# Router tokens turned by transfers and VectorE, the projection evicted by ScalarE, and new ranks in the planner

## Chip, cores and metric

The kernel runs on one core of one Trainium2 chip. The metric is device time in microseconds (us) of one execution.

## What is computed

For 32 sequences of 512 tokens with 256 features, in float32: a pre-normalised attention layer with a residual, then a pre-normalised routed slot layer with a residual.

```python
x = x + attn(layernorm(x));  x = x + ffn(layernorm(x))

# attn
q = tanh(x @ W_charge.T + b_charge)[..., 0]
phi_c = mags * q[..., None] ** arange(5)                 # powers 0..4 of the charge
shell = x @ W_shell.T + b_shell;  shell = shell / norm(shell)
phi_s = concat([cos(shell @ omega.T + rff_bias), sin(...)]) * rff_scale
phi = (phi_c[..., :, None] * phi_s[..., None, :]).reshape(b, n, -1) @ W_combine.T
attn = softmax(where(causal, phi @ phi.T * T / temp, -inf))
out = (attn @ (x @ W_v.T + b_v)) @ W_out.T + b_out

# ffn (the slots S are the same for every sequence before the update)
h = gelu(concat([x, slot_mean]) @ w1.T + b1)
alpha = top-8 softmax of (h @ w2.T + b2) / (|tau| + 0.1), spread over 64 slots
slot_input = einsum('bts,btd->bsd', alpha, x) / alpha.sum(axis=1)
S_new = gru(slot_input, S)
out = einsum('bts,bsd->btd', alpha, S_new @ wv.T + bv) @ wo.T + bo
```

## The kernel before, in words

The work is cut into 16 groups (g = 0 to 15) of two sequences. A group's x is one tile of 128 partitions by 8 token tiles by 256 features. Each group goes through `features` (L827), `attention` (L1070), `router` (L1218) and `slots` (L1356). TensorE = PE, VectorE = DVE, ScalarE = ACT, GpSimd = POOL, and SP issues nearly all transfers.

- **features.** `statistics` (L716) takes means and variances on VectorE (L724) and finishes on GpSimd. The tokens are turned so that features lie on partitions (xT): in groups 0 and 1 by TensorE (pta, L792), in the others by loading x again in 32-token blocks (xb, `load_x`, L261) and turning the 32x32 blocks on VectorE (L814). TensorE projects (pf, L843) with one weight tile for shell, charge and value columns, 321 in all; for the re-laid tokens a re-laid copy of the weights, wfb, is made by eight transfers. VectorE evicts each product with the scale of the normalisation and all biases in one instruction (sv, L856). The charge is spread by GpSimd (qrep, L879), turned by TensorE (ptq, L900), passed through tanh (L908) and squared (L911) on ScalarE. The shell norm, projection (pp, L979), angle and sine (L1011) follow. The powers 1 to 4 of the charge are four multiplications at L1022, of 512 elements each: powers 1 and 3 on VectorE, 2 and 4 on GpSimd. pph (L1041) combines them, and VectorE makes phi (L1056).
- **attention.** Logits (pl, L1094), row minimum (L1123), exponentials (L1135), transposes (ptp, L1171), their eviction (prT, L1189), values (po, L1177), and the addition to x (L1206). The output projection is folded into the value weights.
- **router.** Statistics again, xm (the normalised tokens, L1228, ScalarE), the transposes ptb (L760, inside `transposed`, L750) with evictions by ScalarE (xmT, L772), the hidden layer ph (L1254), gelu (L1265), logits prr (L1279), their transposes prt (L1285), the eight largest (top and rest, L1310 and L1311), the subtraction of the largest (L1319), exponential (L1328), sums (L1335) and weights al on GpSimd (L1344).
- **slots.** psi (L1367) gathers tokens into slots, gi (L1381), the gates prz and pn (L1416), the new state hn on VectorE, ScalarE and GpSimd, then pv (L1503), py (L1523), the addition to x (L1537) and the store (L1542).

The order in which each engine runs is fixed before the launch by a planner (`Plan.order`, L135). Every step has a cost and, for transfers, a time to land. A step's rank is

```python
s.rank = s.g * STRIDE + s.at + DELAY[s.stage]
```

where `at` is the earliest start within its group and the stages are setup, features, attention, router and slots. The planner places the ready step that can start first, by rank where several can, and counts the free buffers of each tag in `SLOTS_OF`. Each engine, and SP as a queue of transfers, then runs its steps in that order; groups overlap, so that one stretch of TensorE holds pf of one group, po of the one before and psi of the one before that.

## Time and profile before

| | us |
|---|---|
| median of 3 runs (lowest, highest) | 747.95 (746.84, 750.34) |
| the profiled execution | 746.77 |
| its span, first to last instruction | 744.9 |

The profile is of that one execution. PE is matmul, PEld weight loading, which overlaps PE; a line such as L760 is a line of the kernel. In a row of groups the columns are busy time, mean ns of one instruction, and idle time before it with what ended it. In a row of one tile's instructions the three numbers are the shortest, median and longest duration in ns. The slices divide the span into 40 parts, each digit a busy share in tenths; PEclk is TensorE's granted clock in tenths. The mean granted clock is 0.973. Matmul durations overlap, because matmuls are pipelined: 64 runs of four transposes ptb have a busy sum of 34.4 us.

### The profile page before, as it was taken

To read this page: it belongs to the slowest core of one execution; us is meant where nothing else is said; L and a number is where in the kernel's file an instruction comes from. 1 tells how busy PE (TensorE), PEld (TensorE's weight loads), DVE (VectorE), ACT (ScalarE), POOL (GpSimd) and SP (SyncE) were. 2 spreads that over 40 slices of the span, in tenths; PEclk is the share of its full clock that TensorE was granted. 3 is DMA by queue.
4 is the path that set the end of the run, shared out by engine and by line. 5 is a ranking of instruction groups with operands and counts; after the bars stand their busy time and mean duration, and the time that the engine had idled before them with its cause. 6 is when DMAs were issued, how large, how long until landed. Compare 5 with 4: busy or idle time off the path is not lost.

```text
span 744.9 us, 12365 instructions
## 1 busy us (share of the span) xinstructions
PE 698.8 (94%) x4170; PEld 489.6 (66%) x4170; DVE 592.2 (79%) x1747; ACT 432.7 (58%) x872; POOL 266.6 (36%) x510
## 2 busy tenths in 40 slices
PE   4988999999999999999999999999999999989754
PEld 4756766776767677677667677677667676756432
DVE  4899758788888889897979899897979788676443
ACT  3235656567475747477585757577585756574520
POOL 6542632342524252341525253442524252402010
PEclk8989999999999999999999999999999999999967
DMA  7886202005070604142150604142030301010103
GB/s 190 225 156 139 56 2 58 1 19 153 1 170 0 165 7 113 58 81 91 35 136 1 166 5 113 57 89 84 1 114 1 114 1 57 0 58 1 58 4 110
DMA packets 99151, 53.76 MB, mean 72 GB/s; under 512 B 63088, under 2 KB 98256, under 8 KB 99088
## 3 DMA queue, kind: packets, MB, share of 16 engines
q1 hardware_dynamic: 97216, 52.02, 27.1%
q8 instruction: 33, 0.54, 0.3%
q10 hardware_dynamic: 1376, 0.62, 0.3%
q0 software_dynamic: 496, 0.33, 0.2%
q14 instruction: 30, 0.25, 0.1%
HBM read 35.85 MB, written 16.78 MB: 71 GB/s over the span
## 4 chain that ended last, share of the span: by engine, by line
PE 76%; DVE 11%; DMA 4%; ACT 3%; SPq 2%; POOL 2%; issue 1%; DVEq 0%; POOLq 0%; ACTq 0%
PE po L1177 17%; PE pf L843 13%; PE ph L1254 7%; PE ptp L1171 4%; PE psi L1367 4%; PE pl L1094 4%; PE prz L1416 4%; PE pph L1041 4%; PE py L1523 4%; PE ptb L760 2%; SPq L247 2%; PE prr L1279 2%; DVE rest L1311 2%; PE pv L1503 2%; PE pn L1416 2%
## 5 line engine op out<-in xcount | busy, mean ns | idle before, releaser
L1177 PE MATMUL po<-sv,prT 128*128 128x256 f32 x640 | 149.6, 380 | 1.2 <-ACT prT L1189 1.2
L1177 PEld LDWEIGHTS po<-sv,prT 128*128 128x128 f32 x640 | 116.8, 189 | 22.2 <-issue 4.7
L843 PE MATMUL pf<-wfb,xT 128*128 128x321 f32 x448 | 126.7, 436 | 0.0
L843 PEld LDWEIGHTS pf<-wfb,xT 128*128 128x128 f32 x448 | 83.0, 189 | 41.4 <-issue 5.9
L1228 ACT ACTIVATE xm<-x,lnb 128x256 f32<-128x256 f32 x128 | 65.7, 590 | 32.8 <-POOL lnb L745 31.2
L1022 POOL TENSOR_TENSOR tp<-tp,q 128x512 f32<-128x512 f32 x32 | 45.4, 1420 | 107.5 <-ACT tp L1011 106.2
L1135 ACT ACTIVATE pr<-lg,nm 128x256 f32<-128x256 f32 (+3 forms) x128 | 70.7, 555 | 17.3 <-DVE nm L1123 16.8
L1206 DVE SCALAR_TENSOR_TENSOR x<-po,den,x 128x256 f32<-128x256 f32 x128 | 58.6, 474 | 20.2 <-PE po L1177 19.6
L856 DVE SCALAR_TENSOR_TENSOR sv<-pf,lna,bias_f 128x321 f32<-128x321 f32 x128 | 64.2, 540 | 13.0 <-PE pf L843 12.9
L1189 ACT COPY prT<-ptp 128x384 f32<-128x384 f32 (+1 forms) x96 | 47.7, 516 | 42.5 <-PE ptp L1171 42.2
L1123 DVE CUSTOM_DVE_ANT_0 lg<-pl,mask 128x128 f32<-128x128 f32 (+3 forms) x128 | 57.2, 483 | 14.0 <-PE pl L1094 9.3
L1254 PE MATMUL ph<-xmT,w1x 128*128 128x512 f32 x128 | 61.5, 606 | 0.0
L1462 POOL TENSOR_TENSOR nn<-nn,rh 128x256 f32<-128x256 f32 x16 | 11.7, 729 | 139.2 <-DVE rh L1453 122.2
L724 DVE BATCH_NORM_STATS2 bna<-x 128x6 f32<-128x256 f32 x128 | 46.4, 409 | 12.3 <-DMA x<-in_x_dram 12.3
L1171 PE MATMUL ptp<-ident,pr 128*128 128x128 f32 x320 | 48.9, 275 | 2.4 <-ACT pr L1135 2.3
L879 POOL COPY qrep<-sv 128x128 f32<-128x128 f32 x64 | 19.6, 321 | 80.6 <-DVE sv L856 79.3
L724 DVE BATCH_NORM_STATS2 bnb<-x 128x6 f32<-128x256 f32 x128 | 47.4, 411 | 0.7
L1171 PEld LDWEIGHTS ptp<-ident,pr 128*128 128x128 f32 x320 | 38.1, 140 | 14.4 <-issue 4.3
L1094 PE MATMUL pl<-phi 64*128 64x256 f32 (+1 forms) x384 | 44.3, 359 | 0.0
L1537 DVE TENSOR_TENSOR x<-py,x 128x512 f32<-128x512 f32 x64 | 39.8, 678 | 5.3 <-PE py L1523 5.2
L1094 PEld LDWEIGHTS pl<-phi 64*128 64x128 f32 x384 | 31.2, 186 | 11.2 <-issue 5.1
L1041 PE MATMUL pph<-tp,wc 64*64 64x256 f32 x640 | 38.2, 381 | 0.0
(177 smaller groups left out, 1339.7 us busy)
## 6 DMA issues: line engine op xcount, KB each, us to landing
x<-in_x_dram SPq DMA_DIRECT2D x32, 512.0 KB, 4.9
out_dram<-x SPq DMA_DIRECT2D x64, 256.0 KB, 2.5
xb<-in_x_dram SPq DMA_DIRECT2D x112, 128.0 KB, 3.4
setup<-in_gru_whh_t_dram SPq DMA_DIRECT2D x1, 768.0 KB, 4.6
wih<-in_gru_wih_t_dram SPq DMA_DIRECT2D x1, 768.0 KB, 6.4
wfb<-wf SPq DMA_DIRECT2D x8, 40.1 KB, 2.5
setup<-in_W_v_dram ACTq DMA_DIRECT2D x1, 256.0 KB, 8.7
setup<-in_W_out_t_dram ACTq DMA_DIRECT2D x1, 256.0 KB, 8.8
```

The source lines that it names most:

```text
L724: lambda t=t: nc.vector.bn_stats(st()[:, t, :], src()[:, t, :]),
L843: nc.tensor.matmul(pf()[:, 0:NF], tile_()[:, k, c * P : (c + 1) * P], w[:, k, :], start=(k == 0), stop=(k == KD - 1),)
L856: lambda t=t, pf=pf: nc.vector.scalar_tensor_tensor(sv()[:, t, :], pf()[:, 0:NF], ln()[:, 1, t : t + 1], bias_f, ALU.mult, ALU.add,),
L1041: nc.tensor.matmul(phs[h]()[bb * COMB : (bb + 1) * COMB, 0:HT], wc[r, m, :], tp()[r, m, bb * HT : (bb + 1) * HT], start=(m == 0), stop=(m ...
L1094: nc.tensor.matmul(pls[bb]()[:, off[i] + lo : off[i] + lo + w], phi()[r, 0, q : q + P], phi()[r, 1, k : k + w], start=True, stop=True,)
L1123: nc.vector.tensor_tensor_reduce(out=lg()[:, c], in0=pls[bb]()[:, c], in1=mask[:, T - w : T], scale=1.0, scalar=TOP, op0=ALU.add, op1=ALU.min,
L1135: nc.scalar.activation(pr()[:, c], lg()[:, c], AF.Exp, bias=nm(), scale=-1.0, accum_out=den()[:, tiles.index(i), bb : bb + 1],)
L1171: nc.tensor.transpose(pt()[:, j : j + P], prs[bb]()[:, j : j + P], ident)
L1177: nc.tensor.matmul(po()[:, d * D : (d + 1) * D], pr_t()[:, lo : lo + P], sv()[:, bb * NT + j, C_V:NF], start=(j == 0), stop=(j == i),)
L1206: nc.vector.scalar_tensor_tensor(xt()[:, t, :], po()[:, d * D : (d + 1) * D], den()[:, d, bb : bb + 1], xt()[:, t, :], ALU.mult, ALU.add,)
L1228: lambda t=t: nc.scalar.activation(xm()[:, t, 0:D], xt()[:, t, :], AF.Identity, bias=ln()[:, 4, t : t + 1], scale=ln()[:, 1, t : t + 1],),
L1254: nc.tensor.matmul(ph(), w1x[:, k, :], tiles[k](), start=(k == 0), stop=(k == KD - 1))
```

## The change

- The router's tokens: xm is laid out in four feature quarters of 64, each with a column of ones. In groups 0 to 13, 16 transfers on SP for each of a group's two sequences move 32-partition pieces of xm into xmT (4 token tiles by 65 elements, 1,040 bytes a partition), and VectorE turns the 32x32 blocks in place, two instructions of 512 elements a sequence. ph then uses re-laid weights w1b (four more loads at the start), reads xmT in runs of 32 elements, and gelu writes its output in token order again. psi is 260 columns wide instead of 257. Groups 14 and 15 (`LAST_BY_TENSOR`) keep transposing on TensorE with evictions on ScalarE.
- The projection is evicted by ScalarE, with the scale alone. GpSimd adds the value bias to x (two instructions of 1024 elements a group; attention weights sum to one, so the bias passes through), VectorE adds the shell bias (two instructions a group), and the charge bias goes into the tanh.
- The four powers become two VectorE instructions of 1024 elements.
- The planner: twelve stages instead of five, each with two delays (the second for the last groups), ranks that mix the earliest start with the length of what follows (`LATE`), new constants, some costs, and fewer buffers for xT, xmT, row and half.

The diff, cut to its core:

```diff
@@ -54,8 +57,8 @@
-    "xT": 4,
-    "xmT": 4,
+    "xT": 3,
+    "xmT": 3,
@@ -64,17 +67,31 @@
-    "row": 8,
-    "half": 5,
+    "row": 6,
+    "half": 4,
 }
 HOP = 0.5
 TABLE = 1.28
-SWITCH = 2.0
-STRIDE = 26.0
-
-DELAY = {"setup": 0.0, "features": -32.0, "attention": -14.0, "router": -1.0, "slots": 3.0}
+SWITCH = 0.94
+STRIDE = 33.46
+LATE = 0.77
+
+DELAY = {
+    "setup": (0.0, 0.0),
+    "load": (17.9, 6.2),
+    "tokens": (0.9, -4.2),
+    "angles": (-26.7, -8.1),
+    "phi": (1.6, 1.1),
+    "weights": (5.2, 7.7),
+    "values": (-6.7, -0.6),
+    "normal": (23.4, 21.8),
+    "router": (17.0, -4.1),
+    "taken": (5.8, -10.8),
+    "gru": (31.9, -18.4),
+    "given": (38.2, -0.7),
+}
@@ -143,8 +160,23 @@
                 ),
                 default=0.0,
             )
+
+        for s in reversed(self.steps):
+            s.tail = (
+                s.cost
+                + s.land
+                + max(
+                    (o.tail + (HOP if o.eng != s.eng else 0.0) for o in s.next if o.g == s.g),
+                    default=0.0,
+                )
+            )
+        last = max(s.g for s in self.steps)
+        longest = max(s.tail for s in self.steps if s.rank is None)
+        for s in self.steps:
             if s.rank is None:
-                s.rank = s.g * STRIDE + s.at + DELAY[s.stage]
+                at = (1.0 - LATE) * s.at + LATE * (longest - s.tail)
+                delay, late = DELAY[s.stage]
+                s.rank = s.g * STRIDE + at + delay + late * max(0, s.g - last + 3)
         free = {e: 0.0 for e in ("PE", "DVE", "ACT", "POOL", "SP")}
         slots = {tag: [0.0] * n for tag, n in SLOTS_OF.items()}
         for s in self.steps:
@@ -613,6 +646,10 @@
+    w1q = a["w1_t"][0:D, :].rearrange("(q k i) n -> q i k n", q=NQ, k=KD)
+    l_w1b = [
+        load("SP", w1b[q * SQ : (q + 1) * SQ, :, :], w1q[q], 32, rank=30.0) for q in range(NQ)
+    ]
@@ -851,21 +860,48 @@
             s = add("PE", 1.1, project, done[c // 2] + w_done, [tile_, pf, sv])
             s_sv.append(
                 add(
-                    "DVE",
-                    0.42,
-                    lambda t=t, pf=pf: nc.vector.scalar_tensor_tensor(
-                        sv()[:, t, :],
-                        pf()[:, 0:NF],
-                        ln()[:, 1, t : t + 1],
-                        bias_f,
-                        ALU.mult,
-                        ALU.add,
+                    "ACT",
+                    0.47,
+                    lambda t=t, pf=pf: nc.scalar.activation(
+                        sv()[:, t, :], pf()[:, 0:NF], AF.Copy, scale=ln()[:, 1, t : t + 1]
                     ),
-                    [s, s_ln] + B_PF,
+                    [s, s_ln],
                     [pf, sv, ln],
                 )
             )
+        s_xb = [
+            add(
+                "POOL",
+                2.9,
+                lambda bb=bb: nc.gpsimd.tensor_tensor(
+                    xt()[:, bb * NT : (bb + 1) * NT, :],
+                    xt()[:, bb * NT : (bb + 1) * NT, :],
+                    bias_f[:, C_V:NF].unsqueeze(1).to_broadcast([P, NT, D]),
+                    ALU.add,
+                ),
+                [s_ln] + (x_t[bb][1][0] if g < BY_TENSOR else []) + B_PF,
+                [xt],
+            )
+            for bb in range(GB)
+        ]
+        s_sh = [
+            add(
+                "DVE",
+                0.4,
+                lambda bb=bb: nc.vector.tensor_tensor(
+                    sv()[:, bb * NT : (bb + 1) * NT, 0:SHELL],
+                    sv()[:, bb * NT : (bb + 1) * NT, 0:SHELL],
+                    bias_f[:, 0:SHELL].unsqueeze(1).to_broadcast([P, NT, SHELL]),
+                    ALU.add,
+                ),
+                s_sv[bb * NT : (bb + 1) * NT] + B_PF,
+                [sv],
+            )
+            for bb in range(GB)
+        ]
+
+        plan.stage = "angles"
@@ -903,12 +939,23 @@
                     ident,
                 )
-        s = add("PE", 0.44, charges_turned, s_rep + [s_ident], [qrep, ptq, qb])
-        s_qb = add(
-            "ACT", 0.6, lambda: nc.scalar.activation(qb(), ptq(), AF.Tanh), [s], [ptq, qb], "exp"
-        )
-        s_q2 = add(
-            "ACT", 0.6, lambda: nc.scalar.activation(q2(), qb(), AF.Square), [s_qb], [qb, q2]
+        s = add("PE", 0.44, charges_turned, s_rep + [s_ident], [qrep, ptq, tp])
+        s = add(
+            "ACT",
+            0.6,
+            lambda: nc.scalar.activation(
+                tp()[:, ORDER + 1, :], ptq(), AF.Tanh, bias=bias_f[:, C_Q : C_Q + 1]
+            ),
+            [s] + B_PF,
+            [ptq, tp],
+            "exp",
+        )
+        s_q = add(
+            "ACT",
+            0.6,
+            lambda: nc.scalar.activation(tp()[:, ORDER + 2, :], tp()[:, ORDER + 1, :], AF.Square),
+            [s],
+            [tp],
         )
@@ -1004,32 +1050,29 @@
             nc.vector.scalar_tensor_tensor(turn(), turn(), -ROUND, ang(), ALU.add, ALU.subtract)
         s = add("DVE", 1.05, nearest, s, [ang, turn])
-        s_tp = {}
-        s_tp[0] = add(
-            "ACT",
-            0.6,
-            lambda: nc.scalar.activation(tp()[:, 0, :], turn(), AF.Sin, scale=-TWO_PI),
-            [s],
-            [turn, tp],
-            "sin",
-        )
-
-        def power(eng, cost, m, by, s_by):
-            e = nc.vector if eng == "DVE" else nc.gpsimd
-            s_tp[m] = add(
-                eng,
-                cost,
-                lambda: e.tensor_tensor(
-                    tp()[:, m, :], tp()[:, m - 1 if by is qb else m - 2, :], by(), ALU.mult
-                ),
-                [s_tp[m - 1 if by is qb else m - 2], s_by],
-                [tp, by],
-            )
-
-        power("DVE", 0.75, 1, qb, s_qb)
-        power("POOL", 1.2, 2, q2, s_q2)
-        power("DVE", 0.75, 3, q2, s_q2)
-        power("POOL", 1.2, 4, q2, s_q2)
+        s_tp = [
+            add(
+                "ACT",
+                0.6,
+                lambda: nc.scalar.activation(tp()[:, 0, :], turn(), AF.Sin, scale=-TWO_PI),
+                [s],
+                [turn, tp],
+                "sin",
+            )
+        ]
+
+        for m in (1, 3):
+
+            def powers(m=m):
+                a, b = tp()[:, 0:1, :], tp()[:, ORDER + 1 : ORDER + 3, :]
+                if m == 1:
+                    a = a.to_broadcast([P, 2, T])
+                else:
+                    a, b = tp()[:, 1:3, :], b[:, 1:2, :].to_broadcast([P, 2, T])
+                nc.vector.tensor_tensor(tp()[:, m : m + 2, :], a, b, ALU.mult)
+
+            s_tp.append(add("DVE", 1.3, powers, [s_tp[-1], s_q], [tp]))
+        plan.stage = "phi"
@@ -1212,32 +1257,108 @@
                             ALU.add,
                         )
-                    s_x[t] = add("DVE", 0.42, added, [s_po, s_den], [po, den, xt])
+                    s_x[t] = add("DVE", 0.42, added, [s_po, s_den, s_xb[bb]], [po, den, xt])
         return s_x
...
+
+
+        by_tensor = g >= NG - LAST_BY_TENSOR
         xm = Lazy("xm", lambda: xms[g % len(xms)])
         al = lazy("al", f"al_{g}", [P, NT, GB, SLOTS])
+
...
         ln, s_ln = statistics(g, "b", xt, [xt], s_x)
+        ones = [s_one]
+        if by_tensor:
+            ones = [
+                add("POOL", 0.2, lambda: nc.gpsimd.memset(plain()[:, :, D : D + 1], 1.0), [s_one, s_ln], [xm])
+            ]
+
...
         s_xm = [
...
+            add("ACT", 0.51, lambda t=t: normalised(t), [s_ln] + ones, [xm, xt, ln])
             for t in range(GT)
         ]
-        xm_t = transposed(g, "b", xm, [xm], s_xm, "xmT")
+
+        xm_t, s_xmt = [], []
+        for bb in range(GB):
+            dst = lazy("xmT", f"xmT_{g}_{bb}", [P, NT * NT, EQ + 1])
+            xm_t.append(dst)
+            here = s_xm[bb * NT : (bb + 1) * NT]
+            done = []
+            if by_tensor:
...
+            else:
+
+
+                moved = [
+                    add(
+                        "SP",
+                        0.45,
+                        lambda bb=bb, q=q, b=b, dst=dst: nc.sync.dma_start(
+                            out=dst()[q * SQ : (q + 1) * SQ, b * NT : (b + 1) * NT, :],
+                            in_=xm()[b * SQ : (b + 1) * SQ, q, bb * NT : (bb + 1) * NT, :],
+                        ),
+                        here,
+                        [xm, dst],
+                        land=2.3,
+                    )
+                    for b in range(NT)
+                    for q in range(NQ)
+                ]
+                for h in range(2):
+
+                    def turn(h=h, dst=dst):
+                        n = NT * NT // 2
+                        v = dst()[:, h * n : (h + 1) * n, 0:EQ]
+                        nc.vector.transpose(v, v)
+
+                    done.append(add("DVE", 0.63, turn, moved, [dst]))
+            s_xmt.append(done)
+        plan.stage = "router"
@@ -1247,27 +1368,25 @@
...
-                    nc.tensor.matmul(
-                        ph(), w1x[:, k, :], tiles[k](), start=(k == 0), stop=(k == KD - 1)
-                    )
-
-            s = add(
-                "PE", 1.72, hidden, [xm_t[bb, k][1] for k in range(KD)] + [l_w1x], tiles + [ph, h_t]
-            )
-            s_h.append(
-                add(
-                    "ACT",
-                    0.6,
-                    lambda ph=ph, h_t=h_t: nc.scalar.activation(h_t(), ph(), AF.Gelu, bias=b1e),
-                    [s, s_b1e],
-                    [ph, h_t],
-                    "gelu",
-                )
-            )
+                    if by_tensor:
+                        w = w1x
+                        rhs = tile_().rearrange("p t e -> p (t e)")[:, k * T : (k + 1) * T]
+                    else:
+                        w = w1b
+                        rhs = tile_()[:, :, k * SQ : (k + 1) * SQ]
+                    nc.tensor.matmul(ph(), w[:, k, :], rhs, start=(k == 0), stop=(k == KD - 1))
+
+            def active(ph=ph, h_t=h_t):
+                src, dst = ph(), h_t()
+                if not by_tensor:
+                    src = src.rearrange("p (b c i) -> p b c i", b=NT, c=NT)
+                    dst = dst.rearrange("p (c b i) -> p b c i", b=NT, c=NT)
+                nc.scalar.activation(dst, src, AF.Gelu, bias=b1e)
+
+            s = add("PE", 1.72, hidden, s_xmt[bb] + [l_w1x] + l_w1b, [xm_t[bb], ph, h_t])
+            s_h.append(add("ACT", 0.6, active, [s, s_b1e], [ph, h_t], "gelu"))
             h_ts.append(h_t)
```

## The prediction, on record before the run

> **What bounds the kernel now.** I read the busy shares and the slices first, then the chain of waits, then busy time by stretches, then the groups with their forms.
>
> ```profile
> PE 698.8 (94%) x4170; PEld 489.6 (66%) x4170; DVE 592.2 (79%) x1747; ACT 432.7 (58%) x872; POOL 266.6 (36%) x510
> PE   4988999999999999999999999999999999989754
> PEclk8989999999999999999999999999999999999967
> PE 76%; DVE 11%; DMA 4%; ACT 3%; SPq 2%; POOL 2%; issue 1%; DVEq 0%; POOLq 0%; ACTq 0%
> ```
>
> TensorE is never below nine tenths between the first 90 us and the last 60, at a full clock, and three quarters of the chain is TensorE work. The middle falls only with TensorE's work; the two ends fall with latency.
>
> ```profile
> 279.00:372.00 93.00, 93.00 (x562) 66.14 (x561) 81.34 (x241) 59.79 (x120) 35.41 (x71) 1.00 0.29 75
> sum 372.00, PE 370.91 PEld 261.09 DVE 319.96 ACT 237.91 POOL 141.12; mean PE 92.73 PEld 65.27 DVE 79.99 ACT 59.48 POOL 35.28
> ```
>
> The columns are PE, PEld, DVE, ACT, POOL; the second line sums four stretches from 186 to 558 us. PE is idle 1.1 us of 372. The pph step of group 3 starts at 145.5 us and that of group 15 at 646.2, so a group takes 500.7/12 = 41.7 us. VectorE works 86% of it, 35.9 us; ScalarE 64%, 26.7; GpSimd 38%, 15.8. So VectorE is next in line.
>
> **The change part by part.** *Router transposes off TensorE.* Busy times of single matmuls overlap, so the price is the time a run holds the chain (start, us, what):
>
> ```profile
> 158.31 1.75 PE ptb L760 x16
> L772 ACT COPY xmT<-ptb 128x512 f32<-128x512 f32 x64 | 33.3, 593 | 0.6 <-PE ptb L760 0.4
> L814 DVE STREAM_TRANSPOSE xT<-xb 128x512 f32<-128x512 f32 x56 | 36.8, 686 | 0.0
> L247 SPq DMA_DIRECT2D wfb<-wf x8: 534/589/650, 19.9 to 24.4; - x8
> DMA to landing us min/median/max: 1.9/2.5/3.3
> ```
>
> Groups 0 to 13 lose 16 transposes each: 14 x 1.75 = **24.5 us of TensorE work**, all on the bounding engine; groups 14 and 15 keep theirs. ScalarE loses 4 x 0.52 = 2.1 us a group. VectorE gains 4 turns of 512 elements, at 36.8/56: 2.6 us. SP gains 32 transfers a group. The nearest row is wfb: also SBUF to SBUF, 32 partitions, 1.3 KB a partition against 1.04 here. At 0.589 us that is 18.8 us of SP; beside it stand 8 xb loads (5.0 us in the timeline), 4 stores (2.2) and 2 x loads (0.9): 26.9 of 41.7, so SP has room, but in order. In the new order 12 or 13 of item 1's 16 transfers stand before the stores of group g-2 and the rest behind them, so these wait for VectorE's last addition there; behind them wait the next xb and x loads.
>
> Does the longer road fit? In the new order TensorE has about 31 us of work between the last po of a group and its first ph. The road is addition and statistics 0.9, GpSimd's statistics 3.7, eight xm 4.1, 16 transfers 9.4, landing 2.5, two turns 1.3: 22 us. The second item's last transfers: from py to the second ph, TensorE has about 14 us, the road is 0.5 + four additions 2.5 + stores 2.2 + four transfers 2.4 + landing 2.5 + turns 1.3 = 11.4. Cover left: 9 and 2.6 us. The second is thin.
>
> ph now reads its moving side in pieces of 32 elements. No row shows that. Bounds: nothing, or a tenth of ph's 3.44 us a group (4.8 us in all); nothing can be gained, since the columns stay the same. I take nothing, because psi, pf and ph rows differ only with their columns. Permuted xm and gelu outputs on ScalarE: same answer, hidden by its idle 13 us.
>
> *Projection evicted by ScalarE.* Eight copies of 321 elements a group, nearest row prT 128x384 at 482 ns: +3.9 us on ScalarE, which comes to 26.7 - 2.1 + 3.9 = 28.5 us. VectorE loses 64.2/16 = 4.0 us and gains two additions for the shell bias; the shn row (128x256, 14.4/32) gives 0.9 us.
>
> *Powers and value bias.*
>
> ```profile
> L1022 POOL TENSOR_TENSOR tp<-tp,q x32: 1264/1310/1775, 47.5 to 640.5; 128x512 f32<-128x512 f32 x32
> L1022 DVE TENSOR_TENSOR tp<-tp,qb x16: 676/1322/1687, 46.3 to 639.5; 128x512 f32<-128x512 f32 x16
> L1022 DVE TENSOR_TENSOR tp<-tp,q x16: 691/1640/1653, 47.0 to 641.0; 128x512 f32<-128x512 f32 x16
> L1319 DVE TENSOR_TENSOR rl<-rl,top 128x512 f32<-128x512 f32 x16 | 11.6, 727 | 0.6
> L918 POOL TENSOR_TENSOR sq<-sv 128x256 f32<-128x256 f32 x32 | 19.7, 616 | 0.0
> ```
>
> The same multiplication takes VectorE 0.68 us at best and 1.64 when GpSimd multiplies beside it. The Trainium skill (SBUF — State Buffer, "Who interferes with whom") has the rule: a VectorE instruction with two SBUF inputs and a GpSimd instruction that reads SBUF shut each other out for a whole instruction. The rows agree with the waiting. For the powers this speaks for the change: VectorE loses 2.6 us (41.6/16) and gains two instructions of 1024 elements at 2 x 0.727 = 2.9, GpSimd loses 2.8. For the value bias the rule speaks against it: two additions of 1024 elements, 4 x 0.616 = 2.5 us each by the sq row, 2.8 by the powers row. In the new order they stand behind GpSimd's first statistics, when VectorE comes to the subtraction of the largest, the new state and the shell bias, all with two SBUF inputs. By the busy rows alone it costs VectorE nothing; by the rule one to two instructions wait up to 2.5 us a group. I take 1.3 to 2.5.
>
> VectorE's sum a group: 35.9 - 4.0 - 2.6 + 2.6 + 0.9 + 2.9 = 35.7, with the lock 37 to 38.2. TensorE's: 41.7 - 1.75 = 39.9. TensorE still bounds, but VectorE is at 93 to 96% and its queue is in order. For what then shows through (turns waiting for landings, the lock, fewer row and xT buffers) I take 0.33 us a group, **+4 us** over 12; the bounds are 0 and 5.
>
> *The planner.* Changes of TensorE's tile mode: 195 before, 189 after, so nothing there.
>
> Start: x of group 1 was loaded second and its transposes ran at 13.7 and 16.2 us, in time that TensorE had to wait anyway. Now its loads stand behind wfb, whose issue ends at 25 us; with 4.9 us to land, those transposes come at 30, behind pf of group 0: **+3.5 us**.
>
> End, by the timeline of TensorE:
>
> ```profile
> 678.22 3.62 PE L1177 MATMUL po<-sv,prT 128*128 128x256 f32 x16
> 704.40 0.60 PE L1285 MATMUL prt<-ident,rlT 128*128 128x128 f32 x4
> 716.42 0.66 PE L1391 MATMUL pt_hn<-ident,hn 128*128 128x128 f32 x2 [11.42 <-DVE hn L1477]
> ```
>
> From the last po (681.8) to the end are 63 us of group 15's own latency, with holes of 11.4 and 4.2 us. The new order puts more work under it: ph of group 14 (3.44), prz and pn of 13 (2.6) and half of ptb of 14 (0.87). **6.9 us** leave the stretch before. Against it ScalarE does the two gelu steps of group 14 inside the last chain and VectorE hn and x of 13: **+2 us**.
>
> Sum: -24.5 - 6.9 + 3.5 + 2 + 4 = -21.9 us. The profiled execution took 746.77 us (744.9 of span, 1.9 around it), 1.2 below the median of the runs. I take the difference from the median: 747.95 - 21.9 = 726.0.
>
> **The rivals.**
>
> *A, TensorE stays the bound (0.56): 726*, own range 716 to 735.
>
> *B, VectorE becomes the bound (0.18).* If the lock costs 5 us (each GpSimd addition holds one instruction for its whole length), VectorE has 40.7 us of work; with a few tenths of waits a group takes 41. Twelve groups then gain 0.7 each, 8.4, plus 1.4 net from the ends (6.9 - 3.5 - 2) less 2 at the edges of the middle: about 740. For it: 86% busy now. Against it: the sum above.
>
> *C, slower (0.10): the turned tokens come late.* VectorE waits at the turn of xmT with all its other work queued behind, then TensorE at ph. If landings beside xb loads take 4.9 us as for x, not 2.5, and VectorE is 3 us behind at the additions before the stores, the road of 11.4 becomes 16.8, 2.8 more than its cover. 12 x (2.8 - 0.33) = 30 us on A: 755. It ends slower from 2.2 us of lateness a group. Against it: the order leaves room on SP, and the wfb row landed in 2.5 us in a crowded stretch.
>
> *D, the ends gain more (0.13): 711.* TensorE is idle 16 us in the first 93 and 26 in the last 94; if group 1's late x costs nothing and the stalls before the last po (5 us) close, 726 - 3.5 - 5 - 4 - 2 = 711.5.
>
> *E, the change doesn't do what it says (0.03): ph costs more* for its short pieces, by up to a fifth: 14 x 0.69 = 10 us, 736.
>
> **How the numbers follow.** A measurement here tells 0.5% (3.7 us) from no change. A, D and E are faster; of B I give 0.14 to faster and 0.04 to no change; of C 0.01 to no change and 0.09 to slower. Faster 0.86, same 0.05, slower 0.09. The range goes from below D, 706, to where no change begins, 744; about 0.05 lies below and 0.13 above.
>
> **What would show it.** TensorE's busy time about 25 us lower and still full in the middle; a group at 40.2 us between pph steps; VectorE about 90% or more there; the tp row of VectorE near 1.45 us for 1024 elements; GpSimd's x row near 2.5; SP 0.5 to 0.6 per xmT transfer. Wrong: TensorE idle in the middle with VectorE's turn or DMA as releaser (C), VectorE full with rows of two SBUF inputs stretched (B), the ph row above 592 ns (E).

## The result and the profile after

| | us |
|---|---|
| before, median of 10 runs (lowest, highest) | 748.5 (746.8, 751.7) |
| after, median of 10 runs (lowest, highest) | 744.5 (740.7, 749.0) |
| after, the profiled execution, its span | 740.65, 738.9 |
| ratio of after to before, 95% interval | 0.9938 (0.9910 to 0.9966) |

The kernel became 4 us faster where 22 were forecast, and 744.5 lies just outside the range. The direction was right, the size was not. The profiled execution is the fastest of the ten after the change, 3.8 us below their median, and that of the kernel before lies 1.7 below its own, so the traces differ by 6 us where the medians differ by 4. Here are the busy shares, the slices and the chain of waits of the changed kernel:

```profile
PE 682.3 (92%) x3946; PEld 465.7 (63%) x3946; DVE 596.3 (81%) x1707; ACT 454.9 (62%) x939; POOL 291.1 (39%) x512
PE   5989898899999898999989998999989989899885
PEclk8998999999999999999999999999999999999997
PE 47%; DVE 19%; DMA 9%; ACT 9%; SPq 7%; POOL 5%; issue 3%; ACTq 0%; DVEq 0%; POOLq 0%
```

The work has moved as planned: TensorE is 16.5 us less busy, ScalarE 22.2 and GpSimd 24.5 us more, VectorE about as before. But TensorE has 8s in the middle, where it had none before, and its share of the chain fell from 76% to 47%. The same stretches of the middle, in the same columns, say it in numbers:

```profile
372.00:465.00 93.00, 87.37 (x521) 59.99 (x521) 84.43 (x224) 60.15 (x126) 38.82 (x64) 0.98 0.40 96
sum 372.00, PE 354.97 PEld 243.26 DVE 330.09 ACT 240.64 POOL 153.21; mean PE 88.74 PEld 60.82 DVE 82.52 ACT 60.16 POOL 38.30
```

TensorE idles 17.0 of 372 us, against 1.1 before, and the granted clock is 0.98 where it was 1.00. VectorE idles too, so neither engine is full. Between the pph steps of groups 3 and 13, a group takes 42.28 us, against 41.79 before and 40.2 in the forecast. By stretches, cut at the starts of those two steps and at the end of the last po:

| us | before | after | difference |
|---|---|---|---|
| start to pph of group 3 | 145.4 | 151.0 | +5.6 |
| ten groups | 417.9 | 422.8 | +4.9 |
| pph of group 13 to the last po | 118.5 | 109.0 | -9.5 |
| last po to the end | 63.1 | 56.1 | -7.0 |

The ends gained what was expected of them, more or less. The ten groups should have gained 15 us (41.7 to 40.2 each) and lost 4.9, so it is there that one has to look. The waits of TensorE over those 372 us of the changed kernel name what ended them (us in all, how often, the longest):

```profile
PE pt_hn L1521 <- DVE hn L1608: 11.8, 6, 2.2
PE pl L1138 <- ACT sv L865: 4.7, 3, 1.8
```

So TensorE stands at one place of its order, right behind the projection pf: at the transposes of the new state (pt_hn) in six groups and at the logits (pl) in three others. The timeline shows how hn came late (start, duration, what; a row may hold several instructions):

```profile
328.55 4.40 POOL L877 TENSOR_TENSOR x<-x,bias_f 128x1024 f32<-128x1024 f32 x2
```

```profile
328.82 2.28 DVE L1438 TENSOR_TENSOR rl<-rl,top 128x512 f32<-128x512 f32 x1
331.02 2.22 DVE L1607 SCALAR_TENSOR_TENSOR rh<-rz,rh 128x256 f32<-128x256 f32 x1
333.27 0.43 DVE L1608 SCALAR_TENSOR_TENSOR hn<-rh,nn 128x256 f32<-128x256 f32 x1
```

```profile
321.27 2.39 PE L1084 MATMUL pph<-tp,wc 64*64 64x256 f32 x40
323.59 0.66 PE L1404 MATMUL prt<-ident,rlT 128*128 128x128 f32 x4
324.08 7.74 PE L852 MATMUL pf<-wfb,xT 128*128 128x321 f32 x28
333.84 0.41 PE L1521 MATMUL pt_hn<-ident,hn 128*128 128x128 f32 x2 [2.02 <-DVE hn L1608]
```

GpSimd starts the first of its two additions 0.27 us before VectorE's subtraction rl, and rl, 0.73 us on average before, ends 0.55 us after the first addition; rh, 0.42 before, ends 0.28 us after the second. hn comes at 333.7, TensorE has been through with pf since 331.8. This row of the kernel before shows what rh took without the additions:

```profile
L1476 DVE SCALAR_TENSOR_TENSOR rh<-rz,rh 128x256 f32<-128x256 f32 x16 | 6.7, 416 | 3.3 <-POOL rh L1470 3.3
```

The chain of waits confirms the path, in order of time; an instruction that overlaps the one before it counts there only from where that one ends:

```profile
321.34 2.39 PE pph L1084 x40
323.73 1.40 DVE phi L1099 x4
325.13 0.15 DVE top L1429
...
328.82 2.28 DVE rl L1438
331.10 2.15 DVE rh L1607
...
333.27 0.44 DVE hn L1608
```

From pph over phi, the eight takes of the top, rl, rh and hn, VectorE's in-order queue makes one chain, although hn doesn't depend on phi or on the top. Beside it TensorE has only prt and pf to do.

### The profile page after: what moved, and what is told of

Same layout as the page of the kernel before. It is cut to its first block, busy times and chain, and to the rows that moved or that the text cites. A ratio compares the mean times of both kernels' runs of the same rounds, so it can differ in the third digit from the quotient of the medians.

```text
span 738.9 us, 12845 instructions
## 1 busy us (share of the span) xinstructions
PE 682.3 (92%) x3946; PEld 465.7 (63%) x3946; DVE 596.3 (81%) x1707; ACT 454.9 (62%) x939; POOL 291.1 (39%) x512
## 4 chain that ended last, share of the span: by engine, by line
PE 47%; DVE 19%; DMA 9%; ACT 9%; SPq 7%; POOL 5%; issue 3%; ACTq 0%; DVEq 0%; POOLq 0%
PE po L1222 12%; SPq L1341 5%; DMA x<-in_x_dram 5%; PE ph L1379 4%; PE pl L1138 4%; PE py L1655 4%; PE psi L1491 3%; PE prz L1547 3%; PE ptp L1216 3%; ACT xm L1291 3%; PE pf L852 3%; PE pph L1084 3%; DVE rest L1430 2%; PE pv L1635 2%; DVE rh L1607 2%
## 5 line engine op out<-in xcount | busy, mean ns | idle before, releaser
L1179 ACT ACTIVATE pr<-lg,nm 128x512 f32<-128x512 f32 (+3 forms) x128 | 70.9, 558 | 20.3 <-DVE nm L1167 20.2
L865 ACT ACTIVATE sv<-pf,lna 128x321 f32<-128x321 f32 x128 | 60.1, 528 | 19.9 <-PE pf L852 19.6
L877 POOL TENSOR_TENSOR x<-x,bias_f 128x1024 f32<-128x1024 f32 x32 | 65.7, 2068 | 3.6 <-DVE bias_f L478 3.6
L1357 DVE STREAM_TRANSPOSE xmT<-xmT 128x512 f32<-128x512 f32 x56 | 39.1, 705 | 27.2 <-DMA xmT<-xm 21.7
L1167 DVE CUSTOM_DVE_ANT_0 lg<-pl,mask 128x256 f32<-128x256 f32 (+3 forms) x128 | 55.9, 483 | 6.1 <-PE pl L1138 3.0
L1138 PE MATMUL pl<-phi 64*128 64x256 f32 (+1 forms) x384 | 50.2, 384 | 9.6 <-ACT sv L865 5.4
L761 DVE BATCH_NORM_STATS2 bna<-x 128x6 f32<-128x256 f32 x128 | 45.4, 412 | 16.9 <-DMA x<-in_x_dram 16.8
L1379 PE MATMUL ph<-xmT,w1b 128*128 128x512 f32 x112 | 54.2, 604 | 0.1
L761 DVE BATCH_NORM_STATS2 bnb<-x 128x6 f32<-128x256 f32 x128 | 50.3, 417 | 0.9
L1138 PEld LDWEIGHTS pl<-phi 64*128 64x128 f32 x384 | 35.3, 202 | 23.2 <-ACT sv L865 9.1
L1669 DVE TENSOR_TENSOR x<-py,x 128x512 f32<-128x512 f32 x64 | 40.2, 682 | 5.3 <-PE py L1655 5.3
L822 DVE STREAM_TRANSPOSE xT<-xb 128x512 f32<-128x512 f32 x56 | 37.5, 690 | 2.7 <-PE pf L852 2.7
## 6 DMA issues: line engine op xcount, KB each, us to landing
wfb<-wf SPq DMA_DIRECT2D x8, 40.1 KB, 3.5
```

The costliest lines, as they stand in the source:

```text
L761: lambda t=t: nc.vector.bn_stats(st()[:, t, :], src()[:, t, :]),
L865: lambda t=t, pf=pf: nc.scalar.activation(sv()[:, t, :], pf()[:, 0:NF], AF.Copy, scale=ln()[:, 1, t : t + 1]),
L877: lambda bb=bb: nc.gpsimd.tensor_tensor(xt()[:, bb * NT : (bb + 1) * NT, :], xt()[:, bb * NT : (bb + 1) * NT, :], bias_f[:, C_V:NF].unsque ...
L1138: nc.tensor.matmul(pls[bb]()[:, off[i] + lo : off[i] + lo + w], phi()[r, 0, q : q + P], phi()[r, 1, k : k + w], start=True, stop=True,)
L1167: nc.vector.tensor_tensor_reduce(out=lg()[:, c], in0=pls[bb]()[:, c], in1=mask[:, T - w : T], scale=1.0, scalar=TOP, op0=ALU.add, op1=ALU.min,
L1179: nc.scalar.activation(pr()[:, c], lg()[:, c], AF.Exp, bias=nm(), scale=-1.0, accum_out=den()[:, tiles.index(i), bb : bb + 1],)
```

## The experiments

Two theories stood at first. *Lock*: GpSimd's additions hold VectorE, hn comes late, TensorE waits. *Transfers*: the turned tokens come late. Four kernels were run against both. In the later ones helper functions shift the line numbers by about twenty; the names of the tiles tell what is meant.

### 1. Without the additions

```diff
-                lambda bb=bb: nc.gpsimd.tensor_tensor(
-                    xt()[:, bb * NT : (bb + 1) * NT, :],
...
-                ),
+                lambda: None,
```

> The changed kernel without GpSimd's addition of the value bias to x (the value bias of attention is left out; the order of everything else is the same). Two theories. Lock: these two additions, 2.1 us each, hold up VectorE's two-input instructions behind them (the subtraction of the largest and the new state), TensorE then waits for hn and its clock drops for some us. Then the middle goes to about 40.3 us a group, the PE clock to 1.00 there, and the time to 718 to 729. Transfers: the turned tokens come late and VectorE waits at the turn. Then nothing that matters is taken away and the time stays at 741 to 747.

743.5 us, ratio 0.9915 (0.9888 to 0.9941). The stretched rows are gone (rl 0.69 us, rh 0.42), pt_hn no longer waits for hn, and the time is where it was. The number of *Lock* failed; that of *Transfers* came true, but TensorE does not wait for turned tokens. TensorE now waits in seven groups at the next tile, as the waits of this kernel over the same 372 us say, and the timeline of one such group:

```profile
PE pl L1133 <- ACT sv L865: 9.8, 7, 1.8
```

```profile
287.69 0.70 PE L1133 MATMUL pl<-phi 64*128 64x256 f32 x2
289.86 3.02 PE L1133 MATMUL pl<-phi 64*128 64x256 f32 x14 [1.47 <-ACT sv L865]
```

pl needs PSUM buffers, of which the kernel has eight (`ps`), and the eight products of pf have filled them all; they come free as ScalarE evicts (sv). pl's 14 instructions then took 3.02 us, in other groups some 1.7: the clock is low after the gap (more on that at the end).

### 2. The additions in pieces

```diff
-                lambda bb=bb: nc.gpsimd.tensor_tensor(
...
+                lambda bb=bb: [
+                    nc.gpsimd.tensor_tensor(
+                        xt()[:, t, :], xt()[:, t, :], bias_f[:, C_V:NF], ALU.add
+                    )
+                    for t in range(bb * NT, (bb + 1) * NT)
+                ],
```

> The changed kernel with each GpSimd addition of 1024 elements written as four of 256 in the same place of the order; same work for GpSimd, about 0.6 us each instead of 2.1. Lock held for a whole instruction: VectorE gets in between pieces, its stretched instructions fall from 2.2 us to at most 1.2, and the time goes to 722 to 733. Transfers: no change, 741 to 747. If GpSimd simply takes read bandwidth for as long as it works, pieces don't help either: 741 to 747.

745.8 us, ratio 0.9964 (0.9938 to 0.9990), with the same waits of pl for sv (9.7 us, eight times). Here rh takes 0.57 us on average: what held hn is nearly gone, and as in experiment 1 nothing is won.

### 3. and 4. Each large move undone

The third kernel turns all groups' router tokens by TensorE again (`LAST_BY_TENSOR = 16`). The fourth lets VectorE evict with all biases, without GpSimd's additions and the shell additions. In both the planner makes a new order.

> The changed kernel with the router's tokens turned by TensorE in all 16 groups (the planner orders anew); eviction by ScalarE, GpSimd's additions and the powers stay. Lock: TensorE gets its 24.5 us back and the stalls mostly stay, though VectorE has 2.6 us a group more room: 752 to 766. Transfers: with them gone the stalls go as well, and the time is near the kernel before, 742 to 750.

> The changed kernel with the projection evicted by VectorE with all biases in one instruction as before, and without GpSimd's additions and VectorE's shell additions (the planner orders anew); turned router tokens and powers stay. Lock: no lock, but VectorE has 35.7 - 0.9 + 4.0 = 38.8 us a group against TensorE's 39.9: 727 to 740. Transfers: VectorE has less room for late landings, slower than the changed kernel: 746 to 758.

767.2 us, ratio 1.0239 (1.0216 to 1.0262), and 790.0, ratio 1.0546 (1.0503 to 1.0588). The first speaks against *Transfers*, since without them it is 23 us slower, and lies 1 us above the interval of *Lock*. The second missed both theories by 30 us and more. Neither is a clean subtraction, because the ranks were made for the new work and every engine's order moves.

### 5. to 7. The router's exponential behind the evictions

ScalarE's queue in front of the evictions of experiment 1 looks like this:

```profile
287.37 1.28 ACT L1442 ACT_TABLE_LOAD   x1
288.67 0.72 ACT L1442 ACTIVATE rl<-rl,rtau 128x512 f32<-128x512 f32 x1
289.30 1.35 ACT L865 ACTIVATE sv<-pf,lna 128x321 f32<-128x321 f32 x3
```

The third eviction, which frees pl's second buffer, stands behind a table load and the exponential rl, 2.0 us. The next three kernels put that step behind all eight evictions after the planner is done (without the additions; with them; with them in pieces):

```diff
+    for e in [s for s in order if s.late]:
...
+        moved, held = {e}, [e]
+        for s in order[i + 1 : j + 1]:
+            if any(p in moved for p in s.after) or any(
...
+                moved.add(s)
+                held.append(s)
+        stay = [s for s in order[i + 1 : j + 1] if s not in moved]
+        order[i : j + 1] = stay + held
```

> Leaves out attention's value bias (no GpSimd additions), and puts the router's exponential (with its table load) behind all eight evictions on ScalarE; the other three engines keep their order but for the three VectorE steps that read the exponential. Theory 'two stalls': with the lock gone the remaining idle of TensorE is pl waiting for evictions that stand behind the table load, so both edits together end it: idle of TensorE below 0.4 us a group, no half-clock windows in the middle, period 40.2 to 40.7 us, time 718 to 729. Rival 'late lna': the evictions can't start earlier anyway, since GpSimd's statistics arrive when the eight normalisations end, and the period is set by that; then idle stays near 1 us a group and the time is 738 to 745.

> The changed kernel with only the exponential put behind the evictions; the GpSimd additions stay. Theory 'two stalls': the lock's delay of hn stays, so pt_hn still waits some 1 to 2 us in the same groups and the half-clock windows stay: 736 to 745. Rival 'the queue of ScalarE alone': the exponential was the whole stall, 722 to 732.

> Additions cut into four pieces of 256 elements, and the exponential behind the evictions; computes all of the reference. Theory 'two stalls': pieces shorten a held VectorE instruction to some 0.3 us more, the exponential is out of the way: 722 to 733. Rival 'late lna' or any stall elsewhere: 738 to 746.

760.2 us, ratio 1.0166 (1.0116 to 1.0216); 771.0, 1.0287 (1.0238 to 1.0336); 763.3, 1.0193 (1.0149 to 1.0237). All expectations failed. The wait named did end: in the first of them pl runs without a pause. But the exponential also starts the chain to al, which psi needs, and the timeline has the new wait in nearly every group:

```profile
292.23 0.93 PE L1158 MATMUL pl<-phi 64*128 64x128 f32 x8
296.16 1.10 PE L1512 MATMUL psi<-xm,al 128*64 128x260 f32 x8 [3.00 <-POOL al L1484]
```

So ScalarE's order is not simply wrong: at this place it serves two chains that are both due within a few us. That turned the search to what comes before both of them.

### 8. The old ranks

```diff
+                s.rank = s.g * 26.0 + s.at + OLD[s.stage]
```

> The changed kernel's work with the ranks of the kernel before (stride 26, four delays, the old switch price). Theory 'two stalls': the stalls come from where the new ranks set the evictions, the additions and hn side by side, so other ranks move them but this order was made for other work: 735 to 760, and the waits sit at other tiles. Rival 'stalls come with the work': period and waits as in the changed kernel, 741 to 748, pt_hn still waiting for hn.

The table OLD holds the delays of the kernel before; the buffers stay as few as in the changed kernel. 811.5 us, ratio 1.0831 (1.0785 to 1.0876): slower than either expectation. The new work under the old ranks is 67 us slower than under the new ones, so the ranks are a needed part of the change and not an ornament.

### 9. to 12. The load that comes late

What was late upstream stands in the chain of waits of experiment 1:

```profile
264.39 0.46 SPq L1669
...
264.91 0.51 SPq L1336
...
265.47 0.59 SPq L1336
...
266.10 0.58 SPq L279
...
267.38 4.05 DMA x<-in_x_dram
...
271.45 1.40 DVE bna L761 x4
```

A store, two transfers of xmT, a load of xb, then the load of x for a later group, and VectorE stands until x has landed, since its statistics bna come next in its order. Everything behind bna is late by that wait and by the 1.4 us of bna itself: the additions to x, bnb, nn, then GpSimd's statistics, xm, and the evictions behind xm. SP's and VectorE's timelines of the changed kernel show how thin this is, and those of the kernel before show how it was:

```profile
326.92 18.90 SPq L1341 DMA_DIRECT2D xmT<-xm  x30
345.93 2.13 SPq L1674 DMA_DIRECT2D out_dram<-x  x4
348.11 1.72 SPq L1341 DMA_DIRECT2D xmT<-xm  x2
349.88 1.12 SPq L279 DMA_DIRECT2D xb<-in_x_dram  x2
351.72 0.94 SPq L279 DMA_DIRECT2D x<-in_x_dram  x2
```

```profile
355.83 1.41 DVE L761 BATCH_NORM_STATS2 bna<-x 128x6 f32<-128x256 f32 x4 [0.37 <-DMA x<-in_x_dram]
```

```profile
332.79 2.17 SPq L1542 DMA_DIRECT2D out_dram<-x  x4
337.75 0.93 SPq L247 DMA_DIRECT2D x<-in_x_dram  x2
```

```profile
346.14 0.73 DVE L724 BATCH_NORM_STATS2 bna<-x 128x6 f32<-128x256 f32 x2
```

Before, bna started 8.4 us after the first load of x was issued (5.6 to 9.2 in the groups of the middle), and never waited; after, 4.1 us (3.9 to 5.7), and it waits: 8.3 us in eight groups of the changed kernel over those 372 us, 10.8 in nine groups of experiment 1.

```profile
DVE bna L761 <- DMA x<-in_x_dram: 8.3, 8, 2.4
```

The second four of bna come 7 us later anyway. So a small move on VectorE alone takes the first four out of the way, with their wait: in groups 4 to 13 they are taken together with the last four (`behind` puts a step, and what depends on it, behind another).

```diff
+    for g in range(4, 14):
+        here = [s for s in order if s.stats and s.g == g]
+        for s in here[:-1][::-1]:
+            behind(order, order.index(s), order.index(here[-1]))
```

> Leaves out attention's value bias, and on VectorE takes the first four statistics of the tokens loaded for the next group (in groups 4 to 13) together with the last four, so that VectorE doesn't stop for that load; nothing else is moved. Theory 'late load': in the run without the bias, VectorE stood 9.5 us at these statistics (1.05 a group) because the load is issued late on SP's queue; everything behind it, down to the evictions, then comes about 1 us earlier, pl's wait falls from 1.05 to below 0.4 us a group and the half-clock windows go: 724 to 735. Rival 'ScalarE's queue alone': the evictions are held by the eight normalisations and the table load whatever VectorE does earlier: 740 to 746.

721.5 us, ratio 0.9610 (0.9556 to 0.9665): this expectation held. Here are a stretch and the sum of the middle, and all that TensorE waited for there:

```profile
279.00:372.00 93.00, 93.00 (x566) 64.89 (x565) 82.79 (x255) 65.27 (x142) 31.78 (x66) 1.00 0.41 99
sum 372.00, PE 370.60 PEld 256.39 DVE 326.22 ACT 249.88 POOL 120.31; mean PE 92.65 PEld 64.10 DVE 81.55 ACT 62.47 POOL 30.08
```

```profile
PE pl L1154 <- ACT sv L886: 1.4, 2, 1.1
```

TensorE is full again, its clock is 1.00, and a group takes 39.8 us in five of the ten and 40.2 on average. The table load still stands between the evictions: alone it doesn't make the stall.

The name *late load* says more than this run shows. In the group of the chain above, VectorE needed 10.8 us from the second turn of xmT (267.62) to the end of the last bnb in experiment 1, and 8.7 (from 263.33) in this one: 2.0 less, of which 0.64 is the wait for x and 1.40 the four bna, which now stand behind bnb. No run took away the wait and left the work in its place. Nor does the length of the wait in experiment 1 foretell the stall: after a wait of 0.28 us (441.1) pl stood 1.75 us in the next group, after one of 1.44 (229.5) not at all. Shown is that the place of these four statistics makes the second stall; how much of it the load makes is open.

> The changed kernel with the same move of the statistics; the GpSimd additions stay. The chain that ends at pt_hn runs in each group from pph through phi, the eight takes of the top, rl, rh and hn, and starts on TensorE, so both theories of the load leave it: 739 to 747. If the load were the cause of that wait too: 726 to 735.

With the additions left whole and only the statistics moved: 738.2 us, ratio 0.9846 (0.9794 to 0.9899), 0.8 us below what was expected. pl no longer waits, and pt_hn does in every group:

```profile
PE pt_hn L1542 <- DVE hn L1629: 12.8, 9, 1.9
```

> Computes all of the reference: additions in pieces of 256, the statistics together, and the router's exponential behind four evictions instead of two. If the stalls are the lock, the late load and the table load, each a microsecond or two, all three are eased: 724 to 736. If another chain of the same length stands behind them: 739 to 747.

> Leaves out the value bias; the exponential behind four evictions (two in the changed kernel, all eight in the run where psi then stood 3.0 us for al). Theory 'three chains at one place' (hn, evictions, al): pl no longer waits, al comes 0.95 us later and psi waits 0 to 0.6 us: 728 to 739. Rival 'late load': a ring outside sets 42.3 us a group whatever stands there: 741 to 746.

728.1 us, ratio 0.9705 (0.9661 to 0.9748), for pieces, statistics and the exponential behind four evictions together; 739.0, ratio 0.9856 (0.9797 to 0.9915), for the exponential behind four without additions and without the move of the statistics. The first lies in the interval that was named for all three. The second lies at the very end of the interval that spoke for three chains; pl still waited 10.7 us for sv, so its mechanism failed.

### 13. to 16. What the lock costs by its place

The new state's two instructions are put behind two of the eight takes of the top, out of the additions' reach. Experiment 14 has pieces and statistics together, and leaves the exponential and hn where the change has them.

```diff
+    for e in [s for s in order if s.state]:
+        i = order.index(e)
+        near = [n for n in range(max(0, i - 60), i) if order[n].takes]
+        first = max(order.index(p) for p in e.after) + 1
+        if len(near) == 8 and first < i:
+            order.insert(max(near[1] + 1, first), order.pop(i))
```

> Computes all of the reference, additions of 1024 elements kept: the statistics taken together (groups 4 to 13), and on VectorE the new state's two instructions (rh, hn) behind two of the eight takes of the top instead of behind all eight and rl, 2 us ahead of the additions. Theory 'lock by place': the additions then hold only rl, which feeds the exponential and al; pt_hn no longer waits, psi may wait up to 1.5 us for al: 722 to 734. Rival 'lock by amount': VectorE loses the same 3.4 us a group wherever hn stands, 736 to 742.

> Computes all: additions in pieces of 256 and the statistics together, the exponential where the change has it. If the move of the exponential did nothing in the run that had all three, 725 to 731; if it carried part of it, 732 to 740.

> Computes all: pieces, statistics together, hn behind two takes. TensorE's own work is then the only bound in the middle, 39.9 us a group: 719 to 728. If the pieces' larger GpSimd time (5.24 us for 4.40) makes al or the norm late: 729 to 736.

> Computes all: the changed kernel with only hn moved. Theory 'two chains of like length' (the lock's at pt_hn, the late load's at pl): the second stays as it does without the additions, 739 to 746. If the lock alone made the loss: 722 to 734.

| | us | ratio to before (95%) |
|---|---|---|
| 13, hn first, statistics together | 733.0 | 0.9794 (0.9749 to 0.9840) |
| 14, pieces, statistics together | 725.2 | 0.9691 (0.9648 to 0.9735) |
| 15, pieces, statistics together, hn first | 733.5 | 0.9786 (0.9749 to 0.9823) |
| 16, hn first alone | 751.0 | 1.0020 (1.0002 to 1.0039) |

Experiment 14 is the fastest kernel that keeps the additions, 23 us below the kernel before and 19 below the changed one. Its middle, in windows as above:

```profile
279.00:372.00 93.00, 93.00 (x550) 64.54 (x550) 85.00 (x255) 66.37 (x139) 50.34 (x95) 1.00 0.40 97
sum 372.00, PE 371.73 PEld 256.89 DVE 336.21 ACT 251.12 POOL 174.04; mean PE 92.93 PEld 64.22 DVE 84.05 ACT 62.78 POOL 43.51
```

TensorE idles 0.3 us of 372, a group takes 40.1 us, and rh is held far less:

```profile
L1628 DVE SCALAR_TENSOR_TENSOR rh<-rz,rh 128x256 f32<-128x256 f32 x9 | 7.7, 857 | 0.0
```

The time lies in the interval for an exponential whose place did nothing, as its distance to experiment 11 (728.1) says. Experiments 13, 15 and 16 show why the lock's place matters and why hn first is no cure. pt_hn indeed never waits for hn, but rl, now 0.8 us later and still beside the additions, holds the table load and so the evictions behind it. ScalarE's timeline in experiment 15:

```profile
326.90 0.93 ACT L892 ACTIVATE sv<-pf,lna 128x321 f32<-128x321 f32 x2
328.91 1.28 ACT L1475 ACT_TABLE_LOAD   x1 [1.09 <-DVE rl L1466]
330.21 0.72 ACT L1475 ACTIVATE rl<-rl,rtau 128x512 f32<-128x512 f32 x1
```

pl then waits 0.6 us for sv in each group, 0.8 in experiment 13. For 13 the interval held (733.0 of 722 to 734) and the place named, psi, was wrong. 15 missed its 719 to 728 and fell into the interval of a late al or norm, but for the reason just given. 16 is slower than both intervals for it: hn first alone is worth nothing, and pl waits 16.8 us.

The experiments with the order otherwise unchanged make a table of two causes, median us (the kernel before measured 748.5 beside the changed kernel and 748.9 to 749.1 beside the experiments):

| GpSimd's additions | statistics in place | statistics together |
|---|---|---|
| two of 1024 elements | 744.5 | 738.2 |
| eight of 256 elements | 745.8 | 725.2 |
| none | 743.5 | 721.5 |

Down the left column hardly anything happens (743.5 to 745.8), along the first row 6 us; both together give 19 to 23. Two chains of nearly one length, one through the additions and hn, the other through the first four statistics and the evictions, end at the same place of TensorE's order, and each hides the other.

## Why the prediction was right in direction and wrong in size

- **TensorE's work** was sized rightly: 1.75 us a group forecast, and where TensorE is full again a group takes 40.1 (experiment 14) against 41.79, 1.7 less. The row of ph (604 ns, before 606) shows that pieces of 32 elements cost nothing, so rival E falls. What was too generous is the count of 14 groups: the transposes of two of them (32 of 224) lay ahead of pph of group 3, where TensorE was idle for 16.6 of 145.4 us before, and its busy time there did not fall without them (128.8 before, 129.6 after).
- **The start** was put at +3.5 for x of group 1 and took +5.6; the load is indeed issued at 23.5 us, and the first of its transposes run at 28.9 (30 forecast). The rest was not taken apart.
- **The ends** were right as far as can be told: -6.9 and +2 forecast for the stretch around the last chain, and 9.5 and 7.0 us less in the last two stretches, in which TensorE's removed work of the last groups is contained. Of this I have not separated the parts.
- **Single prices** held: xmT's issue 0.59 us (0.589), its landing 1.9 (2.5 taken), its turn 0.705 (0.66), powers 1.22 (1.45), shell bias 0.43 (0.45), eviction 0.53 (0.48), GpSimd's addition 2.07 (2.5 to 2.8). VectorE's work a group with the lock came to 330.1/372 x 42.28 = 37.5 us, inside the 37 to 38.2.
- **The step that failed** is "For what then shows through ... I take 0.33 us a group, +4 us over 12; the bounds are 0 and 5." Between the changed kernel's ten groups (422.8 us) and those of experiment 14 (401.3) lie 21.5 us, 2.1 a group. The step charged the lock to VectorE's sum, and asked whether the sum fits below TensorE's 39.9. It does. But the price is paid on a chain, pph to pt_hn, that has little slack beside prt and pf: by experiment 1, in which nothing is held, hn was done at 329.4 and pt_hn began at 330.8, so 1.4 us. The three rows of the changed kernel over those 372 us (busy, mean ns | idle before), against means before of 416 ns for rh, 727 for rl and 470 for hn, make 2.2 us more a group:

```profile
L1607 DVE SCALAR_TENSOR_TENSOR rh<-rz,rh 128x256 f32<-128x256 f32 x9 | 14.6, 1618 | 0.0
...
L1438 DVE TENSOR_TENSOR rl<-rl,top 128x512 f32<-128x512 f32 x9 | 10.4, 1159 | 0.3
...
L1608 DVE SCALAR_TENSOR_TENSOR hn<-rh,nn 128x256 f32<-128x256 f32 x9 | 8.9, 985 | 0.3
```

The rule of the Trainium skill (SBUF — State Buffer, "Who interferes with whom") thus described the wait, as the held rows show, and the prediction used it, in the wrong account. The 2.1 us a group are both stalls together, and the term had nothing for the second.

- **The load of x** was seen and not followed: the prediction says that the stores wait and that "behind them wait the next xb and x loads", without asking which instruction of VectorE is next to read x, and how long after. It was bna, 4.1 us after the issue instead of 8.4, and the loads of x in the middle took 5.5 us to land (median; 4.5 before). What that wait alone cost was not separated from the 1.4 us of bna.
- **The rivals.** B named the lock and 740, close by number but by luck: it wanted VectorE full at 40.7 us a group, and VectorE idles 42 of 372 us. C wanted TensorE to wait for xmT (its own sum gives 756, not 755). VectorE waits at that turn 10.2 of 372 us in the changed kernel (4.9 of them put down to xmT's own transfers), and 25.7 (22.1) in experiment 14 with TensorE full: there the wait is free.
- **The planner** made the order by its own prices: 0.45 us for each xmT transfer where the trace has 0.59, a load of x that lands in 3.0 where it took 5.5, and no lock. That the order would be sound with the right prices was not tried.

Whether x comes late for SP's queue or for its slot, the trace can tell in part. The load waits for a slot (the kernel has five for x), and the four stores just ahead of it seem to release it: in five of the nine groups in the middle it is issued 0.1 us or less after the last of them has landed (351.72 after 351.64 in the timeline above), in the others 0.4 to 1.4 us after; before, about 0.1 us after in eight of nine. The stores in turn follow xmT's transfers on the queue at once (345.93 after 345.82). So the queue delays the load mostly by way of the stores; behind them it adds 1.4 us at most. What stays open is how the gain of the moved statistics divides between the load's wait and their own work; an earlier load was not tried.

## What to carry to other kernels

Where several engines run in fixed order, price a contention on the chain that it hits, not on the engine's sum: ask for every stretched instruction what stands behind it on its queue, who waits for that, and how much slack that one has beside the bounding engine. If removing one suspected stall changes nothing, look at which wait has taken its place before dropping the theory: here two stalls of 1 to 2 us ended at one place, removing the one alone was worth 1 us at most and the other alone 6, and both together 19 to 23. And look up the first reader of every load whose place in a queue moves.

## What the runs showed of the hardware

**Short gaps cost TensorE twice.** The granted clock fell to one half for 3.41 us, sometimes for twice that, so that 1.7 or 3.4 us were lost, and mostly after gaps shorter than that. These are all gaps of TensorE of 1 us or more between 150 and 570 us in the 18 traces, and how many had half clock begin at most 3.4 us after their end:

| gap of TensorE, us | gaps | followed by half clock |
|---|---|---|
| 1.0 to 1.4 | 26 | 2 |
| 1.4 to 2.4 | 44 | 29 |
| 2.5 to 3.25 | 31 | 24 |
| above 3.25 | 8 | 8 |

The Trainium skill (TensorE: Matmul & The Clock Gate, "What's actually happening") has a free-running window of 3413 ns, and its advice ("Why this matters for your kernels") is to avoid gaps over about 3 us. The traces agree with the window: in each of them every half-clock stretch begins, and all but the last end, on one grid of 3.413 us (in the changed kernel 206.4, 291.8 and 377.1 us, 25 steps from one to the next). The advice is too mild: gaps of half that length did it 29 times in 44. What counts in these traces is how idle TensorE is within one step of the grid. Of the steps at full clock, none of 2053 with less than 43% idle was followed by half clock, 16 of 30 with 43 to 55%, and 44 of 45 with more. So a gap of 1.75 us within one step is enough, and six of the eight gaps of 3.0 us in experiment 6, cut in two by the grid, did nothing. The loss counts: in experiment 1 the low clock took 12.0 us and the gaps themselves 10.5.

**A held instruction waits for the whole of the other one.** In the changed kernel each VectorE instruction that an addition held ended a fixed time after that addition: rl 0.55 us after, rh and hn 0.28, in every group. In pieces the same three instructions took 0.81, 0.86 and 0.75 us on average (experiment 14). GpSimd is held as well: an addition of 1024 elements took 2.00 us in most cases, and 2.45 where rl came between the two, one of 256 elements 0.63 at best and 0.80 on average in the middle of experiment 14.
